# Four graph layers on one core: k's fourth product by quarters, layer 1's statistics on ScalarE, sums written in place, and a new order of work

## The chip, the cores and the metric

One core of a Trainium2 chip runs the whole kernel. The metric is the device time of one launch in microseconds (us), the median of several runs; the host is not in it. The engines are called by short names: PE is TensorE's matmul, PEld its weight load, DVE is VectorE, ACT is ScalarE, POOL is GpSimd, SP is SyncE, which issues the DMAs. All data are float32.

## The reference, cut to what matters

`x` is 128 graphs of 128 nodes with 512 features, `adj` one 128x128 matrix that all graphs share. Each of the four layers ends in a residual sum and a layer norm over the 512 features:

```python
x = layernorm(x + L0(x, adj, w0, bias))   # norm_adj @ (x @ w0) + bias
x = layernorm(x + L1(x, adj, adj, b))     # see below
x = layernorm(x + L2(x, adj, wq, wk, wv)) # rel = adj.T * (q k^T), rows scaled to norm 1, then rel @ v
x = layernorm(x + L3(x, w3, a, beta, adj))# h = x @ w3; softmax attention over leaky_relu sums; elu
```

With both weights equal to `adj`, L1 adds one value to all 512 features of a row, and the norm behind it takes that away again. So the kernel has no step for L1: its first norm stands for the norms of layers 0 and 1 (a guard with `1.0 + EPS` and `EPS * EPS` in place of `EPS`). "Layer 1's statistics" in this text are the mean and variance of that norm, the kernel's kind `w`.

## The kernel before

The 128 graphs are worked in 32 groups of four (`GB = 4`). In a group, `x(b)` is a 128x512 tile of nodes by features for graph `b`. The main work is four dense products with 512x512 weights, each called by a letter:

- `w`: the aggregate `y` (nodes summed by the normalised adjacency, steps `y..`) times `w0`; added onto `x` by steps `dw..`
- `z`: the turned `x` (`xT`) times `gq`, which is Wq and Wk multiplied once in the setup; then `pr` (steps `r0` to `r3`) and `rel` (`rm`)
- `v`: `xT` times the turned Wv; then `f`/`fa`, rel times v, added onto `x`
- `k`: the turned `x` before layer 3 (`nT`) times `w3`; then `h`, attention times k, and `em`, `ee`, `ea`

Each of these products is a 2x2 block product done with seven block products in place of eight (steps `1` to `7`, in the order 1 2 5 6 7 4 3 or near it). Sums of the left blocks (`sy`, `sx`, `sn`, four each, `Left.sum`, on POOL) and of the weights (once, in the setup) are made ahead. A block product is four matmuls of 128x256 on PE (line 766). Some of the block products are themselves done the same way one level down, "by quarters": seven 128x128 matmuls in place of eight (line 730, `make_small`). That costs: four more small sums on POOL (`Left.small`, steps `l..`), a second PE step that runs after the first (`w18` follows `w1`), a copy between the two on ACT (`b..`, `before`), and three small DVE operations (`e..`, `between`). Before the change `w` and `k` do products 1, 2 and 5 by quarters, `z` and `v` also product 4. PE executes each float32 matmul as two records, so a block product is 8 records, one by quarters 8 and 6.

Then come the norms. The first norm's statistics are on DVE (`stw0` to `stw3`, lines 965 and 966: `bn_stats` and `bn_aggr`); `gw` on ACT makes the guard (lines 1021, 1025), `pow` on POOL the inverse root (line 588) and the shift (line 585), `apw0` to `apw3` on ACT apply it (line 1029). The other two norms take their sums from `fa` and `ea` (an accumulated output), and the squares on ACT (`qv..`, `qk..`, line 1003, which write unneeded values into a dead tile). The turned `x` comes from 32x32 transposes on DVE (`xt`, `nt`, line 674) and an exchange of 16 DMAs (`xd`, `nd`, line 680). The attention tile goes through DRAM (`at`, `aw`, `cat`), as does `rel` (`rt`, `wr`, `cr`).

The order of all steps is written out in the source: a list `HEAD`, then the list `TURN` fourteen times, each time for groups one further on (a turn is one group's worth of every step, taken from six different groups), then `TAIL`. Every engine runs its share of the list in that order and waits at each instruction for its inputs. In `TURN` the number ahead of the dot is the group, relative: `4.w1` starts product `w` of a group, the `z` and `v` steps are those of the group before it (3), `2.` and `1.` are still older. The string tables `SLOTS` say which buffer each new tile takes. The left sums have seven buffers, the small attention tiles (tag `m`) four.

Of the kernel before, what the change touches and what calls it, by code (L numbers as in the profile page):

```python
# [66 lines left out]
    "l1": (
        "010111010101010010101011001101001011010010110100101101001011010010110100101101001011010010"
        "110100110010110011010110100100110"
    ),  # L70
    "l2": (
        "010101010101010010110110110110110110110110110110110110110110110110110110110110110101110101"
        "01"
    ),
    "C": (
        "010101010101011010101011011011011011011011011011011011011011011011011011011011011011011010"
# [3 lines left out]
        "012100212102102012012102012102012102012102012102012102012102012102012102012102102012012010"  # L80
        "2110210"
    ),
    "m": (
        "012301202302301210320100130133212013131201310310213231201012103232120131323021213103232120"
        "131323021213103232120131323021213103232120131323021213103232120131323021213103232120131323"
        "02121310233221302022132020213201210312121203210030"
    ),
    "x": (
        "0123457869789012345768901234576890123457689012345768901234576981032"
    ),  # L90
    "q": (
        "010101010101010001001010101010101010101010101011010101010101010100101010101001010101010101"
        "010101010101010001010101010101010101010101010101010101010101010101010101010101010101010101"
        "010101010101010101010101010101010101010101010101010101010101010101010101010101010101010101"
        "010101010101010101010101010101010101010101010101010101010100010101010101010101010101010101"
        "01010101010101010101010101010101010101010101010101010101010101010101010"
# [3 lines left out]
MIDS = 4  # L100
SUMS = 7
ROOMS = {1: 2, 2: 2}
# [8 lines left out]
0.ld1 2.ld0 0.ld0 2.ld1 1.ld1 1.ld0 s.warm s.deg s.root s.nadj s.adjt s.nadjT 0.y10 0.y01 0.cy10  # L111
1.y10 0.cy01 1.y11 1.cy10 1.y01 1.cy11 0.y11 s.m012_0 1.cy01 3.ld1 s.s00 0.w2 s.m012_1 0.cy11
s.s02 0.bi10 s.m012_3 0.y00 0.bi01 2.y10 s.s01 0.cy00 2.y11 0.bi00 0.w1 s.m05_0 0.sy0 s.s03 2.y00
1.y00 0.bi11 s.m05_1 1.cy00 0.sy2 s.m012_2 0.w5 1.bi10 s.m05_3 0.sy3 0.dw1 s.m05_2 0.w6 0.sy1
0.dw2 s.sk0 1.ly12 s.sk2 s.g1 0.dw6 s.s30 0.w7 s.cg1 1.sy0 s.m312_0 1.bi11 0.dw7 s.m312_1 0.w4
1.bi00 0.dw5 s.bi 0.w3 s.sa1 2.cy10 0.dw4 2.cy00 s.sk1 2.cy11 s.g2 s.sa0 0.dw3 0.stw3 3.y11 1.bi01
0.stw0 s.g5 0.stw1 s.sa2 s.dg2 2.y01 s.s31 1.sy2 0.stw2 1.w2 2.cy01 s.s33 s.g6 0.gw s.sa3 1.bw2
s.m35_0 1.w1 s.cg6 0.pow 1.ew2 s.g7 1.bw1 s.m35_1 2.bi11 1.ew1 0.apw0 0.apw1 1.w28 0.xt0 1.ly5
1.w18 s.cg7 s.sk3 s.la 0.apw2 0.apw3 1.sy1 1.w5 1.dw1 3.ld0 0.xt2 s.g4 1.bw5 0.xt1 2.bi01 0.xt3
s.q11 1.w6 2.bi00 s.cg4 0.xd 1.ew5 s.mg12_0 3.bi11 1.w58 s.dg5 s.q02 s.g3 2.bi10 1.dw6 1.dw2 1.w7  # L120
s.dg3 2.ly12 s.mg12_1 1.dw7 s.mg12_3 1.w4 s.sg0 1.dw5 s.sg2 2.w2 s.sg1 4.ld0 2.w1 s.m312_3 2.bw2
s.sg3 2.ew2 2.bw1 0.z1 0.sx0 s.vt3 s.vt0 0.sx2 s.vt1 2.w28 0.cz1 1.dw4 1.sy3 s.vt2 0.z6 1.stw3
s.vd 0.sx1 1.stw2 1.w3 0.cz6 0.sx3 s.mg4_0 2.sy0 0.z5 2.ew1 1.dw3 2.sy1 0.z7 s.mg4_1 2.ly5 1.stw1
2.w18 s.mg4_3 0.cz7 0.z2 2.sy2 0.dz5 1.stw0 0.z4 0.dz2 1.gw s.mg5_0 s.mg12_2 1.pow s.mg5_2 0.z3
0.cz4 s.mg5_1 s.m35_3 1.apw3 s.mg5_3 3.y10 2.dw1 1.apw2 s.sv0 0.v1 1.apw0 3.bi10 2.dw2 1.apw1
1.xt2 s.sv1 0.v2 0.cv1 1.xt3 0.dz3 0.v6 1.xt0 0.dv2 1.xt1 0.r0 s.sv3 0.cv6 1.xd s.mv5_0 2.w5
s.mv4_0 s.mv5_1 s.mv4_1 s.sv2 0.r1 2.bw5 s.mv4_3 s.mv12_0 0.r2 2.ew5 0.r3 s.mv12_2 s.mv12_1 2.w58
s.mv5_3 s.mv12_3 0.rm 0.v7 s.q10 0.sq0 0.rt 0.sq1 2.w6 0.sq2 s.q12 0.cv7 s.q03 0.sq3 s.q00 0.rp
0.v4 s.q13 0.v5 3.cy11 s.q01 3.cy10 0.wr 2.dw6 0.cv4 4.ld1 3.sy0 s.wt0 s.s32 2.w7 2.sy3 0.cr 0.dv5
s.wt1 s.mv5_2 3.y00 1.sx0 2.dw7 0.v3 s.mg4_2 3.cy00 1.lx12 2.dw5 2.w4 s.mv4_2 0.dv3 0.f3 2.dw4  # L130
3.sy1 0.f1 2.stw2 0.f2 3.bi00 2.stw3 1.v1 0.fa3 1.lx4 0.fa2 1.z1 1.bv1 0.fa1 2.w3 1.bz1 1.ev1
1.lx5 1.ez1 0.f0 1.sx2 1.v5 2.dw3 0.fa0 1.z18 1.sx3 1.bv5 2.stw0 1.v18 0.mnv 1.cz1 1.ev5 1.z5
1.sx1 0.qv2 1.z6 2.stw1 0.qv1 1.cv1 0.qv0 1.z2 1.cz6 1.v6 1.bz2 0.qv3 1.ez2 1.bz5 1.z7 0.gv 2.gw
1.ez5 0.pov 1.cv6 2.pow 1.z28 0.apv3 1.z4 1.cz7 1.dz2 0.apv0 1.z58 0.nt3 2.apw0 1.v2 0.sc00 2.apw2
0.nt0 3.y01 1.bz4 0.sc01 0.apv2 1.v58 3.bi01 1.ez4 3.cy01 1.v7 0.apv1 0.nt2 3.ly5 2.apw1 0.sc10
1.bv2 1.z48 2.apw3 0.nt1 1.v4 1.cv7 3.ly12 1.dz4 0.nd 1.ev2 3.w5 1.bv4 1.dz5 1.v28 3.bw5 0.sc11
1.z3 3.ew5 1.dv2 3.w1 0.sc20 3.w2 1.dz3 3.bw1 0.sc21 3.w58 3.ew1 1.r0 1.r1 0.sc30 3.bw2 1.ev4 1.r2
1.r3 3.ew2 1.v48 0.sc31 3.w18 1.dv4 3.w28 0.pw 3.dw1 1.rm 0.k2 0.sn0 3.dw2 1.sq0 2.xt1 1.sq1 0.sn2
0.pe 2.xt0 0.k1 1.sq2 2.xt2 1.sq3 0.sn3 2.xt3 0.k5 1.rt 0.ck1 2.xd 1.rp 1.dv5 s.m312_2 0.sn1 0.pl3
0.dk2 1.v3 0.pl0 s.m35_2 0.pl1 0.pl2 3.sy2 0.k6 1.dv3 0.ej 3.w6 0.ck6 3.sy3 0.ei 0.ex0 0.k7 3.dw6  # L140
0.ex3 0.ex2 0.ex1 3.w7 0.rd 0.ck7 0.so0 0.dk5 0.so1 4.y11 3.dw7 1.wr 0.k4 3.dw5 4.bi11 0.at 0.aw
2.lx12 3.w4 4.cy11 1.cr 0.ck4 3.w3 3.dw4 2.sx0 3.stw2 0.cat 2.z1 3.stw3 2.sx2 2.z2 3.dw3 2.bz1
3.stw0 1.f2 2.sx1 2.bz2 3.stw1 2.v1 2.lx5 2.ez2 1.f0 3.gw 0.k3 1.fa2 2.bv1 3.pow 1.fa0 2.ez1 1.f1
2.lx4 3.apw0 0.dk3 1.f3 3.apw3 3.xt0 3.apw1 2.z18 1.fa1 3.apw2 0.h0 1.fa3 2.cz1 2.v5 3.xt2 1.mnv
3.xt1 0.h3 1.qv0 2.ev1 2.z28 1.qv1 2.z6 3.xt3 1.qv2 2.dz2 3.xd 1.qv3 0.em3 2.v18 0.em0 2.bv5 1.gv
0.h1 2.cz6 2.ev5 1.pov 0.ee0 2.z7 0.ee3 0.em1 1.apv3 0.ea0 1.apv0 0.ea3 2.v58 2.cz7 2.z5 1.sc00
0.ee1 1.apv1 4.y00 1.sc01 2.bz5 0.ea1 4.y10 1.apv2 4.bi00 2.ez5 4.cy00 4.y01 4.cy10 4.bi10 1.sc10
0.h2 4.cy01 1.sc11 2.z4 4.bi01 2.cv1 0.em2 2.v2 1.sc20 2.bz4 4.sy0 0.ee2 2.z58 2.ez4 2.bv2 2.v6
4.ly12 2.ev2 1.nt1 2.z48 2.cv6 1.sc21 2.v28 2.dz4 2.sx3 2.v7 1.sc30 3.sx0 2.dz5 4.w1 1.sc31 2.cv7
3.lx12 2.dv2 2.z3 1.pw 4.bw1 1.nt2 4.ew1 2.v4 2.dz3 1.pe 4.w18 3.sx2 1.nt0 2.bv4 2.r0 1.nt3 3.lx5  # L150
4.dw1 2.r1 2.ev4 3.z2 4.sy2 0.ea2 2.r2 1.pl3 1.pl0 2.r3 4.sy1 0.mnk 1.pl2 4.w6 1.pl1 3.sx1 2.rm
0.qk3 2.rt 2.sq0 1.ej 2.v48 0.qk2 2.wr 4.dw6 3.z1 2.dv4 1.nd 2.sq1 3.lx4 0.qk1 4.w7 1.ei 2.dv5
3.bz1 1.ex0 3.ez1 1.ex1 2.v3 1.ex3 4.sy3 1.ex2 4.dw7 2.sq2 3.bz2 1.rd 2.sq3 1.so0 3.z18 3.ez2
# [254 lines left out]
def kernel(  # L408
# [43 lines left out]
    def wide(t):  # L452
        return t.rearrange("p a b -> p (a b)")
# [954 lines left out]
```

## Time and profile before

| | us |
|---|---|
| median of 4 runs (1981.95 to 1984.89) | 1982.78 |
| the profiled execution, own time | 1984.29 |
| its span, first to last instruction | 1982.5 |
| PE busy in the span | 1956.0 (99%) |
| PE busy of a 200 us window from 800 on | 200.00 |

The profile lists busy time by engine, groups of instructions by line and shape with the mean of one in ns and the idle time ahead of them, waits with what ended them, and the chain of work that ended last. PE's ends are modelled: a matmul's listed duration (379 ns for 128x256) overlaps the next one's, and what counts is how far the starts lie apart, which the chain shows. Line 579 is `copy` on ACT, 582 `tt` on DVE, 585 `pool_tt` on POOL, which record many different steps; their tile names tell them apart (`p_k`, `q_k`, `l_y`, `S_y`).

### The profile page before, as it was taken

What the parts mean: (1) busy time and instruction counts of PE and PEld (TensorE: products, weight loads), DVE (VectorE), ACT (ScalarE), POOL (GpSimd) and SP (SyncE); (2) the same over time, 40 slices, a digit from 0 to 9 for tenths busy, and PEclk for the clock granted to TensorE, in tenths of its full rate; (3) what the DMA queues carried; (4) which work ended last, traced back from release to release, by engine and by line L of the source; (5) the groups of instructions that cost most, each with busy time, mean ns of one, the idle gap of its engine ahead of it and who ended that gap; (6) DMA issues with size and microseconds to landing.
All of it is one profiled execution on the core that took longest, in us unless ns stands there. A gap on an engine that the chain in (4) does not pass through costs nothing.

```text
span 1982.5 us, 37439 instructions
## 1 busy us (share of the span) xinstructions
PE 1956.0 (99%) x12405; PEld 1724.7 (87%) x12405; DVE 1644.4 (83%) x3801; ACT 1123.9 (57%) x2800; POOL 1369.8 (69%) x1702
## 2 busy tenths in 40 slices
PE   8999999999999999999999999999999999999997
PEld 8888988888888988888988888988889888898885
DVE  7888787888788888888888888888888888787887
ACT  2245556565655656565556556556655556566467
POOL 7557678676686776786766776766877767777652
PEclk9999999999999999999999999999999999999999
DMA  5523455334444445444345453445443454434434
GB/s 203 90 47 63 97 79 135 60 85 102 107 99 85 75 90 107 104 100 74 82 91 113 98 106 57 91 99 112 92 102 59 92 106 102 96 60 108 76 73 107
DMA packets 737312, 184.55 MB, mean 93 GB/s; under 512 B 689376, under 2 KB 689760, under 8 KB 737120
## 3 DMA queue, kind: packets, MB, share of 16 engines
q1 hardware_dynamic: 736976, 182.03, 43.9%
q8 instruction: 100, 1.64, 0.4%
q14 instruction: 92, 0.75, 0.2%
q10 hardware_dynamic: 144, 0.13, 0.0%
HBM read 64.03 MB, written 49.87 MB: 57 GB/s over the span
## 4 chain that ended last, share of the span: by engine, by line
PE 89%; SPq 3%; DVE 2%; DMA 2%; POOL 2%; ACT 1%; issue 1%; POOLq 0%; DVEq 0%; ACTq 0%
PE p_k L766 10%; PE p_w L766 10%; PE p_v L730 9%; PE p_z L730 9%; PE p_v L766 8%; PE p_z L766 7%; PE p_k L730 7%; PE p_w L730 7%; PE pr L1142 5%; PE pl_k L1190 5%; PE pl_v L1190 5%; PE py L935 5%; SPq L680 3%; PE pk L1059 1%; POOL l_x L585 0%
## 5 line engine op out<-in xcount | busy, mean ns | idle before, releaser
L1029 ACT ACTIVATE x<-x,nb,r 128x512 f32<-128x512 f32 x383 | 289.6, 808 | 30.0 <-POOL nb L585 29.4
L585 POOL TENSOR_TENSOR x<-x,bias_bc 128x512 f32<-128x512 f32 x128 | 165.1, 1294 | 121.8 <-PE py L935 92.3
L588 POOL TENSOR_TENSOR r<-v,minus_half 128x4 f32<-128x4 f32 (+1 forms) x99 | 98.8, 999 | 199.7 <-ACT v L1025 188.3
L582 DVE TENSOR_TENSOR x<-p_w,x 128x512 f32<-128x512 f32 x224 | 153.5, 686 | 47.9 <-PE p_w L766 21.8
L1214 DVE SCALAR_TENSOR_TENSOR e<-x,wa_bc 128x512 f32<-128x512 f32 x256 | 172.4, 673 | 1.4 <-ACT x L1029 0.7
L579 ACT COPY C_k<-p_k 128x512 f32<-128x512 f32 x124 | 71.6, 578 | 147.3 <-PE p_k L766 134.9
L935 PE MATMUL py<-nadjT,x 128*128 128x128 f32 x1024 | 135.9, 279 | 1.5 <-DVE x L1310 0.6
L935 PEld LDWEIGHTS py<-nadjT,x 128*128 128x128 f32 x1024 | 127.9, 195 | 5.8 <-DVE x L1310 1.2
L1190 PE MATMUL pl_k<-C_k,attT 128*128 128x512 f32 x248 | 123.0, 594 | 2.0 <-DMA attT<-d_a 1.9
L1190 PE MATMUL pl_v<-C_v,relT 128*128 128x512 f32 x248 | 121.0, 593 | 0.9 <-DMA relT<-d_r 0.9
L766 PE MATMUL p_z<-S_x,gq 128*128 128x256 f32 x512 | 121.4, 380 | 0.3 <-DVE C_z L582 0.3
L766 PE MATMUL p_w<-w,S_y 128*128 128x256 f32 x512 | 121.2, 380 | 0.4 <-DVE x L582 0.4
L766 PE MATMUL p_v<-wvT,S_x 128*128 128x256 f32 x512 | 121.1, 379 | 0.0
L1305 ACT ACTIVATE pl_k<-pl_k 128x512 f32<-128x512 f32 x127 | 73.4, 581 | 82.9 <-DVE x L1302 82.1
L766 PE MATMUL p_k<-w,S_n 128*128 128x256 f32 x496 | 117.3, 379 | 0.0
L582 DVE TENSOR_TENSOR p_z<-p_z,q_z 128x128 f32<-128x128 f32 x248 | 107.3, 433 | 8.5
L582 DVE TENSOR_TENSOR p_v<-p_v,q_v 128x128 f32<-128x128 f32 x248 | 107.3, 433 | 8.5
L1199 DVE SCALAR_TENSOR_TENSOR x<-pl_v,r,x 128x512 f32<-128x512 f32 x128 | 94.5, 746 | 22.3 <-PE pl_v L1190 17.8
L766 PEld LDWEIGHTS p_z<-S_x,gq 128*128 128x128 f32 x512 | 94.1, 190 | 21.4 <-issue 5.9
L582 DVE TENSOR_TENSOR C_v<-p_v,C_v 128x512 f32<-128x512 f32 x127 | 86.4, 681 | 28.2 <-ACT C_v L579 13.5
L766 PEld LDWEIGHTS p_w<-w,S_y 128*128 128x128 f32 x512 | 93.2, 190 | 12.2 <-issue 1.1
L766 PEld LDWEIGHTS p_k<-w,S_n 128*128 128x128 f32 x496 | 91.7, 190 | 14.0 <-issue 2.9
(1627 smaller groups left out, 6244.8 us busy)
## 6 DMA issues: line engine op xcount, KB each, us to landing
x<-in_x_dram SPq DMA_DIRECT2D x64, 512.0 KB, 4.5
out_dram<-x SPq DMA_DIRECT2D x127, 256.0 KB, 2.5
d_r<-ru SPq DMA_DIRECT2D x31, 256.0 KB, 2.0
relT<-d_r SPq DMA_DIRECT2D x124, 64.0 KB, 2.6
s<-d_s SPq DMA_DIRECT2D x31, 256.0 KB, 4.1
d_a<-au SPq DMA_DIRECT2D x31, 256.0 KB, 2.4
attT<-d_a SPq DMA_DIRECT2D x124, 64.0 KB, 4.0
w<-in_L_gnn_weight_dram SPq DMA_DIRECT2D x1, 1024.0 KB, 8.9
```

The costliest lines, as they stand in the source:

```text
L582: nc.vector.tensor_tensor(o, a, b, f)
L585: nc.gpsimd.tensor_tensor(o, a, b, f)
L588: nc.gpsimd.tensor_tensor(o, v, minus_half[:, : v.shape[-1]], ALU.pow)
L730: nc.tensor.matmul(self.banks[i][:, r, bass.ts(c, P)], lhsT=lhsT, rhs=rhs, start=(not then and n == 0), stop=(n == len(steps) - 1), skip_g ...
L766: nc.tensor.matmul(ps[:, j, :], lhsT=lhsT, rhs=rhs, start=(i not in ONTO and j == 0 and kc == 0), stop=(j == 1 and kc == 1), skip_group_ch ...
L935: nc.tensor.matmul(o, lhsT=self.x_chunk(b, kc), rhs=nadjT, start=True, stop=True)
L1029: nc.scalar.activation(xt, xt, AF.Identity, bias=self.nb[k][:, b : b + 1], scale=self.rstd[k][:, b : b + 1],)
L1142: nc.tensor.matmul(self.pr[:, b, :], lhsT=self.whole["z"][:, fc, b // 2, bass.ts(b % 2, P)], rhs=self.xT.chunk(b, fc), start=(fc == 0), st ...
L1190: nc.tensor.matmul(ps, lhsT=left[:, b, :], rhs=self.whole[k][:, b, :], start=True, stop=True)
L1199: nc.vector.scalar_tensor_tensor(xt, self.pf[b], self.rnorm[:, b : b + 1], xt, ALU.mult, ALU.add, accum_out=self.total("v", b),)
L1214: nc.vector.scalar_tensor_tensor(wide(self.e), self.x(b), 1.0, wide(wa_bc[k]), ALU.mult, ALU.mult, accum_out=self.s[:, k, b : b + 1],)
L1305: nc.scalar.activation(self.pz[b], self.pz[b], AF.Exp)
```

## The change

- Product 4 of `k` is done by quarters for groups 1 to 30: `SMALL` gets `"34"`, the setup four more weight sums (`m34_0` to `m34_3`, DVE), each group steps `ln4` (four POOL sums), `k4` (four 128x128 matmuls), `bk4`, `ek4`, `k48` (three matmuls) and `dk4` in place of `k4` (four 128x256 matmuls) and `ck4`.
- The first norm's statistics move from DVE to ACT: `suw0` to `suw3` (an Identity over `x` in place with accumulated sum), `mnw` (two 128x4 operations), `qw0` to `qw3` (squares with accumulated sum, their unneeded values into `y`'s turned tile), and `gw` is left with one operation.
- `y`'s and `n`'s second left sum (`sy1`, `sn1`, the matrix S2) is written over the block that it comes from; so is the third of the small sums for single blocks, except for `x`'s block 4.
- Five buffers for left sums in place of seven, five `m` tiles in place of four, other buffers of the small sums.
- New `HEAD`, `TURN`, `TAIL` and `SLOTS`.

```diff
-    SMALL = tuple(w + i for w in "0gv3" for i in ("12", "5")) + ("g4", "v4")
+    SMALL = tuple(w + i for w in "0gv3" for i in ("12", "5")) + ("g4", "v4", "34")
...
-            self.s[n] = big.tile([P, 2, 2, P], F32, tag="S", name=f"S{n}_{self.name}", bufs=SUMS)
+            if i == 1 and self.name[0] != "x":
+                self.s[n] = A(1, 0)
+            else:
+                self.s[n] = big.tile([P, 2, 2, P], F32, tag="S", name=f"S{n}_{self.name}", bufs=SUMS)
...
-            room = big.tile([P, 4, len(i), P], F32, tag=f"l{len(i)}", name=f"l{i[0]}_{self.name}", bufs=ROOMS[len(i)])
-            s = [room[:, n] for n in range(4)]
+            over = len(i) == 1 and not (i == (4,) and self.name[0] == "x")
+            tag = "l3" if over else f"l{len(i)}"
+            room = big.tile([P, 3 if over else 4, len(i), P], F32, tag=tag, name=f"l{i[0]}_{self.name}", bufs=ROOMS[tag])
+            s = [room[:, n] for n in ((0, 1, 1, 2) if over else range(4))]
+            if over:
+                s[2] = a(1, 0)
...
+        def sum_of(self, k, b):
+            nc.scalar.activation(self.x(b), self.x(b), AF.Identity, accum_out=self.total(k, b))
+
+        def junk(self, k, b):
+            if k == "w":
+                return self.y.aT[:, b].rearrange("p a n -> p (a n)")
+            return wide(self.relT if k == "v" else self.attT)
...
-                wide(self.relT if k == "v" else self.attT),
+                self.junk(k, b),
                 self.x(b),
                 AF.Square,
...
-            if k == "w":
-                self.var_[k] = self.small("v")
-                self.nm[k] = self.small("nm")
-                nc.scalar.mul(self.nm[k], self.mv[k][:, :, 0], -1.0)
-                v, bias, f = self.mv[k][:, :, 1], eps_bc[:, 1:2], 1.0 + EPS
-            else:
-                v, bias, f = self.var_[k], eps_bc[:, 0:1], 1.0
+            v = self.var_[k]
+            bias, f = (eps_bc[:, 1:2], 1.0 + EPS) if k == "w" else (eps_bc[:, 0:1], 1.0)
```

The first part of the turn, before:

```
4.w1 3.xd 2.cv7 0.qk1 4.w2 4.ly5 2.dv4 4.bw1 1.k1 2.dv5 0.qk3 4.ew1 1.k2 4.bw2 0.gk 1.pl0 0.pok
...
3.z2 3.sx3 3.cz1 1.dk5 2.apv1 1.k4 3.lx5 2.apv2 2.nt1 2.apv0 2.nt2 3.z6 2.apv3 2.sc00 1.ck4 2.nt0
```

and after, with the stretch around the new steps and the turn's end:

```
4.w1 0.pok 1.bk2 1.pl3 1.k18 2.dv5 1.pl1 4.bw1 4.sy2 4.w28 1.ek2 0.apk3 2.v3 0.apk2 1.ln5 4.ew1
...
1.ln4 1.ex0 2.f1 1.ex3 1.ex1 4.w6 1.ex2 2.fa1 5.ld1 1.ck7 3.lx12 1.rd 5.ld0 2.f0 4.dw6 4.w5 2.fa0
4.w7 1.so0 4.bw5 2.mnv 4.ew5 2.qv0 3.sx1 3.z1 2.qv1 4.dw7 1.so1 4.w58 2.qv2 1.k4 3.sx0 2.qv3 4.dw5
3.z2 1.at 3.bz1 1.bk4 3.lx4 3.ez1 2.gv 1.aw 4.w4 1.ek4 3.bz2 2.pov 3.z18 4.dw4 1.k48 3.ez2 3.cz1
3.sx2 3.v2 2.apv1 1.dk4 2.apv2 4.w3 3.lx5 2.nt1 3.bv2 2.apv0 2.nt2 4.suw2 3.ev2 3.z28 3.sx3 3.z5
4.suw3 2.sc00 1.cat 3.z6 2.apv3 2.nt0 3.bz5 1.dk5 2.nt3 1.k3 3.cz6 3.dz2 2.nd 2.sc01 4.dw3 3.z4
2.sc10 4.suw0 3.v1 1.dk3 3.bz4 3.v28 3.ez5 4.suw1 3.z7 4.mnw 3.ez4 3.bv1 4.qw0 3.ev1 1.h1 4.qw3
3.z48 2.sc11 3.cz7 3.z58 4.qw2 1.em1 5.y00 3.dz4 4.qw1 2.sc20 3.v18 1.ee1 5.bi00 3.dz5 4.gw 5.y11
...
5.ly12 3.bv4 1.qk3 3.v7 3.ev4 2.pe 2.bk1 1.qk1 2.ek1 3.v48 1.qk2 2.sn2 5.w2 4.xd 3.cv7 5.sy0 1.gk
2.k2 3.dv4 5.bw2 5.ew2
```

## The prediction

> **What bounds the kernel now.** I read the page's first part, then the table of windows, the chain in order of time, the groups by shape, and PE's waits in the first 150 us. The first part says who is full:
>
> ```profile
> PE 1956.0 (99%) x12405; PEld 1724.7 (87%) x12405; DVE 1644.4 (83%) x3801; ACT 1123.9 (57%) x2800; POOL 1369.8 (69%) x1702
> ```
>
> The windows (busy time of PE, PEld, DVE, ACT, POOL, then the granted clock, DMA share and GB/s) say where PE is not:
>
> ```profile
> 0.00:50.00 50.00, 44.85 (x256) 40.05 (x257) 37.86 (x59) 14.09 (x25) 37.37 (x41) 1.00 0.58 205
> 50.00:100.00 50.00, 47.50 (x266) 42.02 (x265) 43.45 (x97) 12.09 (x28) 28.23 (x28) 1.00 0.53 92
> 100.00:150.00 50.00, 49.24 (x313) 43.86 (x313) 40.49 (x95) 22.08 (x55) 30.09 (x38) 1.00 0.29 43
> ...
> 1000.00:1200.00 200.00, 200.00 (x1282) 177.55 (x1281) 167.53 (x385) 116.15 (x288) 142.80 (x181) 1.00 0.46 97
> ...
> 1950.00:1983.00 33.00, 20.85 (x77) 13.88 (x75) 19.85 (x55) 24.40 (x61) 5.86 (x9) 0.85 0.34 112
> ```
>
> By the table's rows from 600 to 1600 us PE is idle for 0.1 us in all. The first 150 us lose 8.4 us, 150 to 600 lose 4.6, the last 33 lose about 11.7, where the last group's chain of small steps runs out. So a change pays by what it takes off PE, and costs what it makes PE wait. The chain (start, length, records) gives the true spacing of matmuls:
>
> ```profile
> 1009.48 1.56 PE p_z L730 x14
> 1011.04 1.73 PE p_k L766 x8
> ...
> 1047.19 1.79 PE p_w L730 x16
> ```
>
> The first line is exactly a product by quarters: 14 records in 1.56 us, 0.112 each. The second is a plain product: 8 records in 1.73, 0.216 each.
>
> **k's fourth product by quarters.** PE loses 1.73 and gains 1.56 in each of groups 1 to 30. By the last row, sixteen small records in 1.79, fourteen are 1.57, so 0.16 to 0.17 us a group, 4.9 us in all. All of it is on the path, since PE is full. Added up by these spacings, the turn is 59.98 us before (the trace repeats every 60.07) and 59.82 after.
>
> [...] The rows above have 0.112 against 0.216 for the same float32 records, nearly in proportion to the columns, so I go by the rows.
>
> The quarters' other work, by k's own rows: DVE 0.28 + 0.30 + 0.57 for the small steps and 0.68 for `dk4`, 1.83 us a group; POOL four sums of 0.457, also 1.83; ACT a copy of 0.36 for one of 0.58. The four weight sums are about 3.9 us of DVE once, spread over the head. Cover: PE's other products.
>
> **Statistics on ACT.** DVE loses 0.677 + 0.182 four times a group, 3.44 us:
>
> ```profile
> L965 DVE BATCH_NORM_STATS2 st_w<-x 128x6 f32<-128x512 f32 x128 | 86.6, 677 | 1.0
> ...
> L966 DVE BATCH_NORM_AGGREGATE mv_w<-st_w 128x2 f32<-128x6 f32 x128 | 23.3, 182 | 4.4
> ```
>
> ACT gains four sums and four squares. The squares are a known form, 0.72 and a read of 0.19, back to back 0.85. The sums are not in this trace; ACT passes over 128x512 run from 0.58 (copy out of PSUM) to 0.81 (`apply`), and I take the square's 0.72 with its read, being nearest in shape, source and accumulator. So 8 x 0.85 = 6.8 us; with the ends for the four sums (0.58 and 0.81, each with the 0.13 that a square's read adds back to back) between 6.2 and 7.2. Per turn, ACT goes from 35.2 to 42, DVE from 50.6 to 49.0, POOL from 43.2 to 45, all under 59.8. None becomes the bound by its sum.
>
> The latency does grow. After the last `dw3` two of the four DVE pairs and two small ACT steps stood ahead of the root: 2 x 0.86 + 0.49 = 2.2 us. Now two sums 1.8, `mnw` 0.4, four squares 3.6, guard 0.3: 6.1. Queued behind them on ACT are `y`'s copies, `ee1` and `apply`; behind `apply` come the transposes and the exchange. The order pays for it: `w3` starts 25.4 us into the turn, not 29.0. And the exchange does not hang on it: `xd` waits for the buffer of the older `xT`, whose last reader `v48` ends at 58.03 of 59.82, against 59.98 of 59.98. In the trace the exchange starts 0.1 us after the turn does, its sixteen issues take 11.1 us, the last lands at 12.7, POOL's `lx12` ends at 16.8, and `z1` runs at 17.3: a margin of half a microsecond that holds in every turn. In the new turn the exchange starts 1.8 us before the turn's start and `z1` is at 18.1. That wait is relaxed by over 2 us; I put the longer statistics at nothing. Without that cover each microsecond late is 32 us in all.
>
> **Sums in place, buffers, places.** The same POOL instructions with another target; the nearest in-place row (`x<-x,bias_bc`) is 1294 ns, the sums into buffers 1275, so 0 to 0.04 us a group, off the path. POOL had waited 38 us for `p_w` and 17 for `p_v` ahead of those sums; that goes, unpaid. `y`'s tile is held until the last square, but the next user of that buffer, `5.cy00`, stands behind the squares on ACT anyway. What the fewer buffers may cost shows in the places where the list leaves little room. The attention round trip loses slack: `cat` to `h1` had some 25 us, now about 8; `cat`'s issues and landings took 6.1 us (1003.9 to 1010.0). Nothing, but with 2 us to spare.
>
> **The new order's ends.** In the first 150 us DVE has 122 us of work, and PE's named waits there (us in total, times, longest) are mostly for it:
>
> ```profile
> PE p_w L766 <- DVE x L582: 2.7, 4, 0.8
> ...
> PE p_z L766 <- DMA x_0T<-sq_x: 1.2, 1, 1.2
> ...
> PE p_w L730 <- DVE p_w L582: 0.4, 1, 0.4
> ```
>
> Three groups' statistics, 10.3 us, leave DVE there and some 3 us of weight sums come. Bounds: all three waits vanish (-4.3), or the unknown order adds as much (+4.3). I take half of DVE's 3.1, -1.5. The last 33 us end on the same steps of group 31, which the quarters leave out: 0, within 1.5 either way.
>
> **The sum.** -4.9 - 1.5 = -6.4. On the profiled execution, 1984.29 (span 1982.5, 1.8 around it), that is 1977.9; it lay 1.5 over the median, so on the median 1982.78 - 6.4 = 1976.4. A measurement here can tell about 0.2%, 4 us, from no change; the limits are 1978.8 and 1986.7.
>
> **Rivals.**
> (a) The new turn makes PE wait, and the kernel is slower. Place: DVE ahead of `k48`. From `w58`'s end at 19.6 us of the turn DVE does `dw5` 0.69, `at` 0.71, `ez1` 1.15 and `ek4` 1.15, and is done at 23.3; PE wants `k48` at 23.8. `at` waits for POOL's `so1`, which I add up to 19.4 (`lx12` from 12.9, 2.9, then `so0` 1.04, `sx1` 1.28, `so1` 1.27), 0.9 before DVE is free. If POOL is over 1.4 us late, PE waits in every group, and 0.16 us a group eats the gain of the quarters, 0.3 makes it measurably slower. One microsecond a group beyond the margin gives 1982.8 - 4.9 + 30 = 2008; 0.4 us gives 1990. For it: margins of half a microsecond. Against: the old turn ran with such a margin at `z1` without one wait in 1000 us. 0.12.
> (b) Only the quarters pay, or little waits of the head eat part: 1982.8 - 4.9 = 1977.9 with nothing at the ends, 1979 to 1986 with 1 to 8 us of new waits like the `attT` ones (1.9 us between 150 and 700). The part over 1978.8 has 0.19.
> (c) The head gains more than half: all waits that DVE, POOL and DMA give between 10 and 600 us are some 10 us; with most gone, 1970. It lies within the faster share.
> (d) The quarters don't save on PE because weight loads bind (PEld 87%): then 0 for them, and the time is 1981 to 1983. Against it is the row "x14 1.56", which already has its 14 loads. 0.03, within "same".
>
> **How the numbers follow.** Faster takes the forecast and (c), 0.69; same is (b)'s rest and (d), 0.19; slower is (a), 0.12. The range runs from 1970.5, (c), to 1984.5, which leaves out (a) and (b)'s worst.
>
> **What would show it.** Right: 14 records of `p_k` for product 4 in 1.56 us; the turn's period at 59.8 to 59.9 with 200.00 busy in a 200 us window; PE's busy time near 1951; ACT near 1340 us, DVE near 1590, POOL near 1425; fewer PE waits for DVE in the first 150 us. Wrong: a period over 60.07, or a PE wait that returns every turn, at `k48` on DVE, at `h1` on `attT`, or at `z1` on `l_x`.

## The result, and the profile after

The changed kernel takes 1986.51 us (median; 1982.33 to 1989.78) where the kernel before takes 1983.40 on the same chips: 1.0015 times as long, 95% interval 1.0010 to 1.0019. The forecast was 1976.4, its range 1970.5 to 1984.5. The forecast said faster; it is 3.1 us slower, little, but the interval leaves out no change.

The page's first part, after:

```profile
PE 1952.9 (99%) x12585; PEld 1725.5 (87%) x12585; DVE 1595.9 (81%) x3669; ACT 1295.3 (65%) x3344; POOL 1424.7 (72%) x1822
```

PE's 1952.9 is near the 1951 that was forecast, DVE's and POOL's times are the forecast ones, ACT has 45 us less than forecast. So the work did what it should; the rest is where PE stood. The table of windows (PE, PEld, DVE, ACT, POOL busy, then the granted clock, DMA share, GB/s):

```profile
0.00:50.00 50.00, 41.87 (x222) 36.15 (x223) 36.13 (x47) 17.85 (x39) 38.38 (x39) 0.97 0.58 207
50.00:100.00 50.00, 47.06 (x267) 41.69 (x266) 39.78 (x84) 17.69 (x45) 23.63 (x27) 1.00 0.41 65
100.00:150.00 50.00, 49.97 (x322) 44.98 (x321) 40.83 (x91) 27.00 (x65) 30.58 (x36) 1.00 0.36 63
1000.00:1200.00 200.00, 200.00 (x1308) 178.04 (x1307) 161.70 (x375) 135.34 (x351) 151.66 (x199) 1.00 0.44 97
1950.00:1983.00 33.00, 22.47 (x81) 14.47 (x79) 21.09 (x58) 25.94 (x64) 5.96 (x9) 0.90 0.35 114
```

The middle is as full as before and does more: 1308 records in 200 us for 1282. The first row has lost 3 us of PE, and its granted clock is 0.97 where it was 1.00. That row is where most of the forecast broke. The chain of work shows one turn, between the same `pr` of two groups, and in it k's fourth product, now in two parts (`k4`, then `k48`):

```profile
1033.23 1.78 PE pr L1167 x16
...
1068.37 0.89 PE p_k L752 x8
...
1072.55 0.67 PE p_k L752 x6
...
1093.14 1.78 PE pr L1167 x16
```

The turn is 59.91 us, for 60.07 before: 0.16 a group, and 0.89 + 0.67 = 1.56 for fourteen records, both as forecast.

To see where the rest went, I split each span into PE's work and its loss. A record's spacing at full clock is 0.1116 us for 128 columns, 0.215 for 256 (the median of both traces is 0.216) and 0.430 for 512, read from these traces; what lies between the starts of two records beyond that is loss: waits, and the half clock too. The 1.4 us ahead of the first record are counted as work.

| us | before | changed | ninth head order (below) |
|---|---|---|---|
| PE's work | 1941.0 | 1936.2 | 1937.1, 0.9 of it added |
| loss, 0 to 100 us | 13.2 | 18.2 | 16.1 |
| loss, 100 to 600 | 10.6 | 7.3 | 6.0 |
| loss, 600 to 1700 | 2.4 | 3.2 | 3.7 |
| loss, 1700 to the last product | 3.8 | 7.8 | 5.9 |
| last product to the end | 11.6 | 9.6 | 9.5 |
| span | 1982.5 | 1982.3 | 1978.3 |

The work fell by 4.8 us. The head lost 5.0 more, the last groups 4.0 more less 2.0 behind the last product, and 100 to 600 us gave back 3.3. With 0.8 more between 600 and 1700 that cancels in this execution, to within 0.3 us. Between kernels that share this tail's order, the loss from 1700 us on lies anywhere from 5.9 to 9.0 in their profiles, so about a microsecond of such a row is scatter. The median of the changed kernel lies 2.2 us above its profiled execution (1984.26) and that of the kernel before 0.9 below its own (1984.29). That difference is the measured 3.1 us: the profiled execution is the fourth fastest of 42, and no trace shows what the slower ones do.

What happened in the head shows in the lists by time (start, length, engine, what). First VectorE, then PE:

```profile
24.28 1.75 DVE L530 TENSOR_TENSOR wk_t<-wk_sb 128x512 f32<-128x512 f32 x1
25.95 0.68 DVE L597 TENSOR_TENSOR x<-p_w,x 128x512 f32<-128x512 f32 x1
```

```profile
26.68 3.30 PE L788 MATMUL p_w<-w_t,S_y 128*128 128x256 f32 x8 [2.23 <-DVE x L597]
```

`w6` of group 0 waits 2.23 us for the addition `dw1`, which the new order put behind `sk0`, a sum of Wk (the first VectorE line). Then `w6`'s eight records take 3.30 us, not 1.89. The window says why, the number behind POOL's count being the clock:

```profile
27.00:30.00 3.00, 2.98 (x8) 1.85 (x6) 1.78 (x3) 0.00 (x0) 2.92 (x4) 0.53 0.64 243
```

The clock was at one half for 3.41 us from 27.20 on. PE's waits in the first 150 us (total, times, longest) have doubled in the line that was forecast to halve:

```profile
PE p_w L788 <- DVE x L597: 5.7, 5, 2.2
```

### The profile page after: what moved, and what is told of

Same layout as the page of the kernel before. It is cut to its first block, busy times and chain, and to the rows that moved or that the text cites. A ratio compares the mean times of both kernels' runs of the same rounds, so it can differ in the third digit from the quotient of the medians.

```text
span 1982.3 us, 38370 instructions
## 1 busy us (share of the span) xinstructions
PE 1952.9 (99%) x12585; PEld 1725.5 (87%) x12585; DVE 1595.9 (81%) x3669; ACT 1295.3 (65%) x3344; POOL 1424.7 (72%) x1822
## 4 chain that ended last, share of the span: by engine, by line
PE 87%; POOL 3%; SPq 2%; DVE 2%; DMA 2%; ACT 2%; issue 1%; ACTq 0%; DVEq 0%; POOLq 0%
PE p_w L788 10%; PE p_z L752 9%; PE p_v L752 9%; PE p_z L788 8%; PE p_k L752 8%; PE p_v L788 8%; PE p_k L788 7%; PE p_w L752 7%; PE py L957 5%; PE pl_v L1215 5%; PE pr L1167 5%; PE pl_k L1215 5%; SPq L702 2%; POOL x L600 1%; DMA s<-d_s 1%
## 5 line engine op out<-in xcount | busy, mean ns | idle before, releaser
L1023 ACT ACTIVATE x<-x 128x512 f32<-128x512 f32 x128 | 79.8, 625 | 57.8 <-DVE x L597 56.9
L597 DVE TENSOR_TENSOR C_v<-p_v,C_v 128x512 f32<-128x512 f32 x127 | 86.9, 685 | 36.4 <-ACT C_v L594 16.7
L597 DVE TENSOR_TENSOR p_k<-p_k,q_k 128x128 f32<-128x128 f32 x240 | 103.8, 433 | 8.3
L788 PEld LDWEIGHTS p_v<-wvT,S_x 128*128 128x128 f32 x512 | 93.0, 190 | 12.7 <-ACT C_v L594 1.5
L594 ACT COPY C_z<-p_z 128x512 f32<-128x512 f32 x97 | 56.6, 583 | 67.2 <-PE p_z L788 36.0
L597 DVE TENSOR_TENSOR C_z<-p_z,C_z 128x512 f32<-128x512 f32 x127 | 86.6, 682 | 14.7 <-PE p_z L788 9.8
L1284 ACT ACTIVATE e<-e,nmax 128x128 f32<-128x128 f32 x128 | 49.8, 391 | 73.5 <-DVE nmax L1278 73.5
```

The costliest lines, as they stand in the source:

```text
L597: nc.vector.tensor_tensor(o, a, b, f)
L788: nc.tensor.matmul(ps[:, j, :], lhsT=lhsT, rhs=rhs, start=(i not in ONTO and j == 0 and kc == 0), stop=(j == 1 and kc == 1), skip_group_ch ...
L1023: nc.scalar.activation(self.x(b), self.x(b), AF.Identity, accum_out=self.total(k, b))
```

## The experiments

The theory after this reading: quarters and statistics are worth what was forecast, and the head's order takes it back, by waits and by the half clock after them. The rivals: the quarters save less, the statistics cost something, the tail is the place, or the head moves nothing. Ratios are to the kernel before on the same chip; each is uncertain by about 0.0009, 1.8 us. Medians of different runs mix in the chips, on which the kernel before takes from 1982.1 to 1983.5. In the orders, `s.` marks a step of the setup, the number ahead of a dot the group; `dw` are the additions that empty a product's bank, `sk`, `sa`, `sg` and `s3` sums of weights.

**Quarters undone (e1).** k's fourth product in one piece again, in the same places; its weight sums, quarter sums and correction go. 

```
-4.bk4  ek4  k48 (quarters)
+4: 8 matmuls n_4 x W3_4, 128x256, in k4's place
```

> The changed kernel with the quarters alone undone: k's fourth product is four 128x256 matmuls again in every group, at the same place of the order, without its small sums, its copy, its three DVE steps and the four weight sums. Theory 'ends' (the quarters save 0.16 us a group on PE as forecast, and the loss sits in the head and the tail of the new order): a turn of 60.05 to 60.1 us in place of 59.91, 4.9 us more on PE, less 1 to 2 us of DVE in the tail and up to 2 in the head, so 1988 to 1990. Rival 'quarters' (their extra steps on DVE, ACT and POOL cost more than PE gains): faster than the changed kernel, 1981 to 1984.

Measured: 1993.69 us, ratio 1.0057 (1.0044 to 1.0069). PE's work is 1940.9, so the quarters take 4.7 off it, against 4.9 in the forecast. The time is above the 1988 to 1990 expected: the turn is 60.45 for 59.91, and on top of 0.17 of work 0.38 us are lost once a turn before a product of v, which waits for an addition, in an order that was made for the quarters. The rival that they cost more than they save falls.

**Statistics back on VectorE (e2).** 

```
-suw: sum on ScalarE; mnw, qw: mean, squares
+suw: bn_stats, bn_aggr on VectorE; mnw, qw: nothing
```

> The changed kernel with the first norm's statistics alone put back on DVE (bn_stats and bn_aggr at the places of the sums; no squares, no mean step). Theory 'ends': the move was free in the turn, so the period stays 59.91 unless DVE now is late (it gains 3.4 us a turn and is at 52.4 of 59.9): 1985 to 1990, with group 0's statistics 4 us shorter but on the busy DVE of the head. Rival 'statistics' (the longer chain on ACT makes waits at the ends): 1981 to 1984.

Measured: 2046.77 us, ratio 1.0326 (1.0311 to 1.0340), far outside both expectations. The turn is 62.20; PE waits for VectorE in each, in this order:

```profile
PE p_k L788 <- DVE C_k L597: 2.9, 3, 1.0
PE p_z L752 <- DVE p_z L597: 1.5, 3, 0.5
```

(window 1000 to 1200 us, where the changed kernel's list of waits is empty). In this order VectorE has no room for its 3.4 us a group, while ScalarE's longer chain makes no wait in the turn. The loss before 100 us is no lower either, 20.6 for 18.2. So the move to ScalarE is not what costs the time; that it costs nothing at the ends isn't shown, since VectorE's load moved with it.

**First head order (e3).** 

```
- ... s.sk0 1.ly12 0.dw1 s.sk2 0.w6 s.s30 ... 0.dw6 0.dw2 0.w7 s.sk1 ... 0.dw7 s.s33 0.w4 1.sy0 0.dw5
+ 0.dw1 (behind 2.y00) ... 0.w6 1.bi01 0.dw6 0.dw2 s.sk0 0.w7 ... 0.dw7 s.sk2 s.s30 s.m05_3 0.w4 s.sk1 1.bi00 0.dw5
```

> The changed kernel with one stretch of the head reordered: on DVE group 0's additions dw1, dw6, dw2, dw7 and dw5 go ahead of the weight sums (sk0, sk2, s30, m05_3, sk1, s31, s33) that stood in front of them. Theory 'ends': PE's waits of 2.2, 0.8 and 1.4 us between 24 and 35 us shrink to under 1.5 in all, and the 3.4 us at half clock that followed them go; 4 to 5 us less, 1981 to 1983, and with less scatter from run to run if the half clock is what differs between runs. Rival 'head moves nothing' (what PE starts earlier it waits for later, at the x exchange or the weight sums that are now later): within 1 us of the changed kernel, 1985.5 to 1987.5.

Measured: 1987.24 us, ratio 1.0022 (1.0013 to 1.0032): no gain. The wait before `w6` is gone and one of 4.62 us stands before `w3`, which waits for `dw5`, now behind slow sums; the half clock lasts 10.24 us. The rival, that the head moves nothing, held here. Whether it moves nothing in any order was open.

**The tail's order (e4).** `dk4` and `dk5` of groups 29 and 30 ahead of group 31's `rb` and score sums.

```
- 29.dk4 30.k48 30.ck7 31.rb 29.dk5 30.ei 29.k3 31.sc11 ... 31.sc20 30.ex2 30.dk5 31.sc21 30.k3
+ 29.dk4 30.k48 30.ck7 29.dk5 30.ei 29.k3 30.dk4 ... 30.dk5 30.ex1 31.rb 30.ex2 31.sc11 30.k3 31.sc20 31.sc21
```

> The changed kernel with one stretch of the tail reordered: on DVE the block sums of groups 29 and 30's k (dk4, dk5) go ahead of the restoring of w3 (rb) and of three attention sums of group 31 (sc11, sc20, sc21). Theory 'ends': PE's waits of 1.4 and 1.2 us ahead of the two k3 products shrink to under 0.5, and 1 to 2 us of it reach the end: 1984.5 to 1985.5. Rival 'DVE's sum bounds the tail' (it is busy without a gap from 1933 to 1950 whatever the order): the same time within 0.5 us, 1986 to 1987.

Measured: 1985.21 us, ratio 1.0010 (1.0001 to 1.0019), which can't be told from the changed kernel. PE's waits from 1930 us on, in this kernel:

```profile
PE pk L1084 <- DVE x L1327: 1.2, 1, 1.2
PE ps L1158 <- DVE e L1239: 1.0, 1, 1.0
PE p_k L752 <- DVE p_k L597: 0.8, 2, 0.6
PE p_k L788 <- DVE C_k L597: 0.3, 1, 0.3
```

The changed kernel has 2.2 us in the last of these lines and 0.3 in the third. There VectorE is busy for 16.50 of the 17 us from 1933 to 1950, so its order there says little more than who waits.

**The same fault put into the kernel before (e8).**

```
- 0.sy3 0.dw1 s.m05_2 0.w6 0.sy1 0.dw2 s.sk0 1.ly12 s.sk2 s.g1 0.dw6
+ 0.sy3 s.m05_2 s.g1 s.sk0 0.dw1 0.w6 0.sy1 0.dw2 1.ly12 s.sk2 0.dw6
```

> The kernel before, with one piece of the changed kernel's head order put into it: dw1 of group 0 stands behind g's sum sk0, which waits for Wk to land at about 21.8 us, and g1 goes ahead of w6. Nothing else is changed. Theory 'head': TensorE gets a wait of 2 to 4 us for VectorE ahead of w6, the granted clock falls to half for at least 3.4 us after it, the loss before 100 us rises from 13.2 to 16 us or more, and the time rises by 2 to 5 us, to 1985 to 1988. Rival 'the head is forgiving': the later start is made up by later waits getting shorter, and the time stays within 1 us of the kernel before.

Measured: 1986.32 us, ratio 1.0015 (1.0005 to 1.0024): the changed kernel's ratio, with its placing of `dw1`, `sk0` and `g1` alone. The wait is longer than the changed kernel's, 4.73 us for 2.23, and stands one product earlier, ahead of `g1`, whose eight records take 3.78 us at the half clock, not 1.97:

```profile
28.64 3.78 PE L766 MATMUL p_g<-wk_sb,wq_sb 128*128 128x256 f32 x8 [4.73 <-DVE x L582]
```

The loss before 100 us rises by 7.2 us and the time by 2.8: over 4 us are made up later. The rival, a forgiving head, falls.

**The waits filled (e7).** Transposes of the identity on PE, results unread, ahead of `w6`, `w7` and `w4`.

```
+ s.fill4 0.w6 ... s.fill2 0.w7 ... s.fill3 0.w4     (fillN: 4N transposes, 128x128)
```

> The changed kernel with 36 extra transposes of the identity on TensorE (results never read) in the places where its head waits: 16 ahead of w6, 8 ahead of w7, 12 ahead of w4 (about 0.11 us each: 1.8, 0.9 and 1.3 us, where the waits were 2.39, 1.20 and 1.51). Group 0's products come no earlier. Theory 'clock': the half granted clock (3.41 us from 27.2 in the changed kernel, 6.8 and 10.2 us in two of its variants) follows from TensorE having stood idle; with the gaps filled the granted clock stays full after the first 15 us, the stretch costs nothing, and the time falls by 1.5 to 4 us to 1982.5 to 1985, with less scatter. Rival 'clock is not tied to the gaps': the half-clock stretch is still there, the time stays at 1986 to 1988 or rises, since the extra transposes delay the products by up to 1 us.

Measured: 1983.13 us, ratio 1.0005 (0.9996 to 1.0014). No half clock before the last product, and a median 3.4 us under the changed kernel's (2.0 by the ratios), though products come no earlier. The two ratios' intervals overlap, so the gain isn't certain.

**Second to fifth head orders (e5, e9 and e10, e11, e12).** Each takes away the longest waits of the one before. e5: the sums of layer 3's weight go to 110 to 135 us, `dw1`, `dw5`, `dw2` behind the first products.

```
+ 2.y00 0.dw1 0.dw5 0.dw2 ... 0.w6 0.w3 0.dw6 0.w7 1.bi01 s.sk0 0.dw3 2.y11 ... 0.dw7 0.w4 s.sk2 s.sa0 ... 0.dw4 s.sk1
+ (at 0.r0 to 0.v5) s.s30 s.s31 s.s33 s.m35_0 s.m312_0 ...
```

> The changed kernel with its head reordered twice over: all the sums of layer 3's weight (s30, s31, s33 and the smaller ones made from them, twelve steps that nothing needs before about 190 us) go from 28 to 60 us to about 110 to 135 us; group 0's additions dw1, dw5 and dw2 stand right behind its first products, w3 goes ahead of w7, and g's sums sk0, sk2, sk1 stand behind dw6, dw7 and dw4. Nothing is added or left out. Theory 'head': the changed kernel's loss before 100 us (18.2 us of TensorE not issuing, against 13.2 in the kernel before) comes from group 0's additions standing behind slow sums, one of which waits for layer 3's weight to land at about 28 us; with these out of the way the waits of TensorE for VectorE before w6, w7, w4 and w3 (2.39, 1.20, 1.51 us) shrink to below 1.5 us in all, no stretch of half granted clock follows, the loss before 100 us is at most 14 us, and the time is 1979 to 1983 us, at or below the kernel before. Rival 'moved again', as in the first reordering: another wait takes the place, the loss stays at 18 us or more, the time at 1985 to 1988. Rival 'displaced': the twelve sums now delay the first groups' attention between 110 and 200 us, the loss of the second 100 us grows by 3 us or more and the time is above 1986.

Measured: 1986.09 us, ratio 1.0011 (1.0002 to 1.0020). VectorE's waits for `x` are down to 1.2 us; GpSimd's took their place, the loss before 100 us is 19.8, and the rival 'moved again' held:

```profile
PE p_g L788 <- POOL S_wq L600: 6.2, 2, 5.0
```

e9: Wq's sums first on GpSimd; e10: the same with e4's tail.

```
+ 0.w6 0.w3 s.g1 0.bi00 0.dw6 ... s.sa0 s.sa1 s.sa2 0.w7 1.ly12
```

> The changed kernel with the second reordering of the head and two more moves, after that one's trace: there the waits before w6, w7, w4 and w3 were gone, but TensorE came to the weight products g5 and g6 before GpSimd had summed Wq for them (waits of 1.35 and 5.20 us), and the clock was halved again. Now GpSimd sums Wq (sa0, sa1, sa2) ahead of group 1's quarter sums, w6 and w3 go ahead of g1 (which waits for Wk to land), and dw6 and w7 follow g1; two of the five sum buffers swap places for it. Nothing is added or left out. Theory 'head': no wait over 1.5 us before 40 us, no stretch of half clock, loss before 100 us at most 13 us, time 1980 to 1983 us, 3 to 5 under the changed kernel. Rival 'displaced': group 1's sums, now 4 us later on GpSimd, make TensorE wait between 45 and 100 us instead; the loss stays above 17 us and the time at 1985 or above.

> The same head, and the tail's order with the additions dk4 and dk5 of groups 29 and 30 ahead of group 31's adjacency and score sums. Theory: the two places add up: the tail alone gave 1.3 us off the changed kernel's median, so this is 0 to 1.5 us below the kernel with the head alone, 1979 to 1982.5 us. Rival: VectorE has no free time between 1933 and 1950 us, so its order there only moves the wait, and the two kernels agree within 0.7 us.

Measured: 1986.09 and 1986.48 us, ratios 1.0010 (1.0001 to 1.0018) and 1.0016 (1.0007 to 1.0025). The tail adds nothing. In e9 the loss before 100 us is 16.7; idle stretches of 2.10 us (at 38 us) and 1.98 (at 212) have 3.41 us of half clock after each.

e11: those two stretches shortened, by order and by eight transposes ahead of `w2`, which all later heads keep.

```
+ s.dg2 s.bi ...   s.fill2 1.w2 ...   3.z18 2.f3
```

> The kernel with the third head order and three more edits aimed at TensorE's longest idle stretches. In the profiles so far the granted clock went to half for 3.41 us or a multiple after every idle stretch of TensorE of 2.06 us or more (9 of 9), after one of two at about 2.0 us, and after none of those of 1.97 us or less; the third head order still had two, 2.10 us at 38.4 (w2 of group 1 waiting for the addition dg2) and 1.98 us at 212.2 (a product waiting for a transposed tile). Now dg2 goes ahead of two slow VectorE steps, 8 extra transposes of the identity (results unread, 0.9 us) stand ahead of that w2, and z's eighth part of group 3 goes ahead of the waiting product f3 of group 2. Theory 'clock': no stretch of half clock before the last product, and the time is 1980 to 1983 us, 3 to 5 us under the changed kernel and at or under the kernel before. Rival 'waits, not clock': the idle time moved once more, another place crosses 2 us, and the time stays at 1985 to 1987.

Measured: 1982.83 us, ratio 1.0003 (0.9994 to 1.0012), 3.7 under the changed kernel (2.4 by the ratios), though one new stretch of 5.72 us, with 6.83 us of half clock, stands before `g4`. e12 takes that away:

```
+ ... s.fill2 1.w2 2.cy00 0.pow 1.sy2 2.bi00 s.sa3 ... s.g7 s.cg7 0.apw3
```

> The kernel with the fourth head order, with its one long idle stretch taken away: there TensorE stood idle for 5.72 us from 43.62, because g4 waited for a bank that ScalarE empties (cg7), ScalarE stood in cg7's way with group 0's normalization (apw), and that waited for GpSimd's 1/sigma (pow) behind group 1's sums, a bias and a sum of Wq. Now cg7 goes ahead of the normalization, and pow goes ahead of sy2, the bias of group 2 and sa3 on GpSimd. Theory 'head': no idle stretch of 2 us before the last product, no half clock, loss before 50 us at most 8 us instead of 12.1, time 1978 to 1981 us, under the kernel before by 2 to 5 us. Rival 'latency is fixed': group 0's chain to its next product has a length of its own, the idle time reappears later in the first 100 us, and the time stays at 1982 to 1984.

Measured: 1985.51 us, ratio 1.0013 (1.0004 to 1.0022). That is above what the theory and the rival gave: stretches of 3.68 and 3.15 us came up behind it, 10.2 us of half clock with them.

**Sixth and seventh (e13, e14).**

```
e13 + 1.sy2 1.ly5 s.sa3 2.bi00 ...   1.dw7 1.w58 1.dw5 s.sg3
e14 + 2.cy01 2.ly12 ... 2.bi00 2.bi10 2.bi11 2.bi01 ...   1.w4 1.sy3 2.dw1 1.dw4 0.sx2 1.w3 s.sg2 0.sx1 1.dw3 s.vt3
```

> The kernel with the fifth head order, with its two long idle stretches taken away by order alone: 3.68 us at 46.67 (w5 of group 1 waiting for a quarter sum on GpSimd that stood behind biases of group 2) and 3.15 us at 66.53 (w4 of group 1 waiting for the addition dw7 behind three sums of g's weight on VectorE). Now ly5 of group 1 and sa3 go ahead of group 2's biases on GpSimd, and dw7 and dw5 of group 1 ahead of those sums on VectorE. Theory 'head': each idle stretch was a placement; without them no half clock before the last product, loss before 100 us at most 15 us instead of 21.1, time 1979 to 1982.5 us. Rival 'latency is fixed': the head has only so much independent work, the idle time and with it a stretch of half clock come back elsewhere before 100 us, and the time stays at 1984 or above.

> The kernel with the sixth head order, whose waits before 50 us were gone (loss 7.5 us there, less than the 9.4 of the kernel before) and which still had two idle stretches, each followed by 3.41 us of half clock: 2.13 us at 52.27 (w2 of group 2 waiting for its quarter sums, behind four biases on GpSimd) and 4.51 us at 66.81 (z1 waiting for the bank that group 1's additions dw4 and dw3 empty, behind sums of g's weight and transposes of Wv on VectorE). Now those biases stand behind ly12 of group 2, and dw4 and dw3 ahead of the sums and transposes. Theory 'head': no idle stretch of 2 us is left and no half clock, loss before 100 us at most 14 us instead of 19.3, time 1977.5 to 1981 us, below the kernel before, so that the head alone explains why the change did not gain what was forecast. Rival 'the head has no more to give': another wait of the same size appears before 120 us and the time stays at 1982 to 1984.

Measured: 1982.93 us, 1.0009 (1.0000 to 1.0018), and 1983.82, 1.0005 (0.9996 to 1.0013). The first 50 us lose 7.5 and 7.8 us, less than the 9.4 before, but 50 to 100 lose 11.8 and 10.4 for 3.8: waits had moved there, and neither kernel is under the one before.

**Filled stretches (e15, e16, e17).** The sixth, fourth and seventh order with transposes in the stretches that were left.

```
e15 + s.fill3 2.w2 ... s.fill7 0.z1        e16 + s.fill9 s.g4        e17 + s.fill6 2.w28 ... s.fill3 0.z5
```

> The sixth head order with extra transposes of the identity on TensorE (results unread) in its two idle stretches: 12 ahead of w2 of group 2 (1.3 of the 2.13 us) and 28 ahead of z1 of group 0 (3.1 of the 4.51 us). The products come no earlier; only the clock can gain. Theory 'clock': no half clock before the last product, and the time falls by 2 to 3.4 us against the sixth order (two stretches of 3.41 us at half), to 1979.5 to 1981.5 us, below the kernel before. Rival 'the half clock costs little, since the products wait anyway': the time stays within 1 us of the sixth order, at 1982 to 1984.

> The fourth head order with 36 extra transposes (4.0 us) in its one idle stretch, 5.72 us ahead of g4, after which its profile showed 6.83 us of half clock. Theory 'clock': no half clock, the time falls by 2 to 3.4 us, from 1982.8 to 1979.5 to 1981 us. Rival: within 1 us of the fourth order.

> The seventh head order with extra transposes in its two idle stretches: 24 ahead of w2's eighth part of group 2 (2.7 of 3.72 us) and 12 ahead of z5 of group 0 (1.3 of 2.59 us). Its profile had one stretch of half clock, 3.41 us, and its unprofiled runs were a microsecond slower than that of the sixth. Theory 'clock': 1.7 to 3 us below the seventh order's 1983.8, at 1980.8 to 1982.1. Rival: within 1 us of the seventh order.

Measured: 1983.01, 1982.50 and 1984.09 us; ratios 1.0002, 1.0001 and 1.0008, each within 0.0009. Against their twins that is +0.1, -0.3 and +0.3 by the medians, -1.4, -0.4 and +0.6 by the ratios, each uncertain by some 2.5 us. None of the three profiles has a half clock before the last product, and no gain shows: taken together, the three rule out the 2 us or more of the theory, but not one of 1 us. In e7 the half clock may have cost up to 3 us, an estimate from its 3.4 by the medians and 2.0 by the ratios.

**Eighth and ninth (e18, e19).** e18 moves `ew2` of group 2, `dw2` and `dw3`; e19 then moves group 1's `dw2` and `dw6`, Wv's transposes and, to make room, some sums of g's weight.

```
e18 + 2.w2 2.bw2 2.ew2 s.sg0 ...   2.dw1 2.dw2 1.dw4 0.sx2 1.w3 0.sx1 1.dw3 s.sg2 s.vt3 s.vt1 s.vt0 s.vt2 s.mg4_0 s.vd
e19 + 1.dw1 1.dw2 2.w2 2.bw2 2.ew2 s.sg0 1.w6 2.w28 1.dw6 2.w1 ...   2.ew1 s.vt3 s.vt1 1.dw7 1.w58 1.dw5 s.vt0 s.vt2 s.vd
```

> The seventh head order with its two idle stretches taken away by order: 3.72 us at 55.22 (w2's eighth part of group 2 waiting for the step ew2 on VectorE, behind three sums of g's weight that took 1.48 to 1.75 us each while GpSimd added six biases) and 2.59 us at 70.49 (z5 of group 0 waiting for the bank that group 2's addition dw2 empties, behind sg2 and four transposes of Wv). Now ew2 stands ahead of those sums, dw2 of group 2 behind dw1, and dw3 of group 1 ahead of sg2. Theory 'placement': loss before 100 us falls from 18.2 to 14 or less, no half clock, time 1979 to 1982 us. Rival 'the head has no more to give': the loss stays at 17 or more and the time at 1982.5 to 1984.5.

> The eighth head order, which had lost 23.2 us before 100 us in two long idle stretches (3.29 us at 56.49, group 2's w1 waiting for a bank that group 1's dw2 and dw6 empty behind three sums of g's weight; 3.71 us at 83.46, v1 waiting for the exchange of Wv's transposes, now started later) with 6.83 us of half clock after each. Now dw2 and dw6 of group 1 go ahead of those sums, and the transposes of Wv and their exchange go some 8 us earlier, as soon as their buffer is free. Theory 'placement': no idle stretch of 2 us, loss before 100 us at most 14 us, time 1979 to 1982 us. Rival 'no more to give': 17 us or more and 1982.5 or above.

Measured: e18 1987.91 us, ratio 1.0023 (1.0014 to 1.0032); e19 **1979.32 us, ratio 0.9980 (0.9971 to 0.9989)**, below both kernels: 3.2 us under the kernel before on its chip, 7.2 under the changed one's median, and its 11 runs lie within 3.0 us where the changed kernel's 42 lie within 7.5. PE's waits from 50 to 100 us, first e18:

```profile
PE p_v L788 <- DMA wvT<-sq_wv: 3.7, 1, 3.7
PE p_w L752 <- DVE x L597: 3.3, 1, 3.3
```

then e19:

```profile
PE p_w L788 <- DVE x L597: 2.3, 1, 2.3
PE p_v L788 <- DVE wvT_t L530: 0.9, 1, 0.9
```

The two differ by nothing but these few places in the order, and by 8.6 us. e18 is slower than either of its expectations: one of its two long waits, for the exchange of Wv's transposes, came of its own moves. e19's loss before 100 us was expected at 14 or less and is 16.1 in its profile, which is its longest run (1980.96) and has one wait of 2.3 us with 6.83 us of half clock. So the time came as the theory 'placement' had it, the loss did not: it lies between the theory and the rival, above the 13.2 of the kernel before. What is shown is that the order of the head alone moves the time by 8.6 us, and that the changed kernel's loss is not one that every order must keep. No run put the larger number of buffers back, but e19 has the changed kernel's few, so they don't force it. That the head's best order has been found isn't shown.

## Why the prediction was wrong, step by step

- **k's fourth product, -4.9: right.** Fourteen records take 1.56 us and the turn is 0.16 us shorter, 4.8 in thirty; counted by the spacings it is 4.7 against e1.
- **Weight loads bind (rival d): fell,** by the same 0.16 us.
- **Statistics on ACT, 0: right in the turn.** 200.00 us busy of 200. The load was put too high: the sum takes 0.625, not 0.72, and sums follow each other every 0.62 us and these squares every 0.71, not every 0.85, since the read lies under the next one. The squares of the other two norms, which all go into one dead tile, still follow every 0.85; why is not shown. ACT gained 171 us, not 216. Sums and squares in the head, and the long form:

```profile
40.12 0.61 ACT L1023 ACTIVATE x<-x 128x512 f32<-128x512 f32 x1
40.65 0.19 ACT L1023 ACTIVATION_READ_ACCUMULATOR x<-x 128x1 f32 x1
...
41.15 0.72 ACT L1033 ACTIVATE y_0T<-x,neg 128x512 f32<-128x512 f32 x1
41.78 0.19 ACT L1033 ACTIVATION_READ_ACCUMULATOR y_0T<-x,neg 128x1 f32 x1
41.87 0.70 ACT L1033 ACTIVATE y_0T<-x,neg 128x512 f32<-128x512 f32 x1
```

```profile
L1033 ACT ACTIVATE attT<-x,neg 128x512 f32<-128x512 f32 x124 | 89.6, 723 | 1.1
...
L1023 ACT ACTIVATE x<-x 128x512 f32<-128x512 f32 x128 | 79.8, 625 | 57.8 <-DVE x L597 56.9 <-DMA wvT<-sq_wv 0.7
```

- **A wait in every turn (rival a): did not come.** PE's list of waits from 1000 to 1200 us is empty.
- **"I take half of DVE's 3.1, -1.5": the step that failed.** It reckoned with VectorE's load and not with where each addition stands. The loss before 100 us rose by 5.0, that of the 150 us that the step spoke of by 3.9 (14.8 to 18.7): 5.4 off, and close to the upper bound given, +4.3. What the step left out could be read in the change's own list: `0.dw1` behind `s.sk0`, a sum that takes 1.75 us here, where the seven of its shape that ran in this trace while GpSimd rested took 0.68. That such a placing is enough, e8 shows: it costs the kernel before 2.8 us. Rival b had the mechanism (new waits in the head) and the size, 1 to 8 us, though its 1986 was just passed, and too little chance.
- **The tail, 0 within 1.5: wrong by 2.0.** 4.0 more loss from 1700 us on, 2.0 less behind the last product. The two waits before `k3` are new, 1.19 and 1.01 us; e4 moved the additions that they wait for ahead and gained nothing that can be told, so what would remove them is open.
- **150 to 600 us were not in the sum.** They gave 2.0 back, which nothing had foreseen; 600 to 1700 took 0.8.
- **Profile and median.** Of the 10.1 us between forecast and result these terms make 6.4, in the profiled executions (1984.26 against 1977.9). The other 3.7 is the step from profile to median: the forecast took off 1.5, and the changed kernel's median lies 2.2 above its profile. 0.6 of it is the baseline, 1982.78 from four runs and 1983.40 from sixty. What the rest is stays open.

With e19's head half of the 6.4 us comes out: 1979.32 against 1982.52 on the same chip. Of its profile's span, 4.2 us under the kernel before's, 3.9 is work; its head still loses 2.9 us more than the kernel before's and its last groups 2.1 more, and 100 to 600 us (4.6) and the end (2.1) make up for that. What also stays open is how much of the changed kernel's 2.2 us between profile and median is the half clock. In its runs the time goes with the mean granted clock, median 1985.2 at 0.999 and 1987.0 at 0.997, but e15 to e17 took the half clock away and no gain showed. A version with e19's head and a better tail was not tried.

## What to carry to other kernels

A load table says whether an engine can be the bound, and nothing of a stretch in which another engine waits for one small step of it: when an order changes, go through the queue ahead of each step that PE waits for, with that stretch's durations and not the turn's. One wait removed often brings up the next behind it, so an order is judged by the time and the whole head's loss, not by the wait that it took away: the first eight reorderings gave from 1.4 us worse to 3.7 better, the ninth 7.2 (by the ratios 1.6, 2.4 and 6.9). Split the span into work and loss by stage before asking why: here the work fell as forecast, and only the loss needed explaining.

## What the runs showed of the hardware

- **The clock falls after short stand-stills.** In the twenty traces, from 12 us to the last product, no idle stretch of PE between 0.95 and 1.97 us was by itself followed by a half clock, 7 of 10 between 1.98 and 2.6 us were (among them 2.23 us in the changed kernel, 2.13 in e13 and 2.34 in e19; 2.59 in e14 was not), and all 12 of 2.9 us and more (3.15 in e12 and 5.72 in e11 among them); it starts 2.3 to 4.8 us after the stretch begins (2.91 in the changed kernel; once 1.0, with a shorter stretch just ahead) and lasts 3.41, 6.83 or 10.24 us. Why the start varies these runs don't show.
- **VectorE's sums of two SBUF tiles mostly slow down while GpSimd works.** The same 128x512 sum (the first and the third line), VectorE first, GpSimd's list after it:

```profile
13.67 0.68 DVE L530 TENSOR_TENSOR w_t<-w,w_t 128x512 f32<-128x512 f32 x1
14.27 1.49 DVE L546 TENSOR_TENSOR m<-w,m 128x256 f32<-128x256 f32 x1
15.69 1.76 DVE L530 TENSOR_TENSOR w_t<-w,w_t 128x512 f32<-128x512 f32 x1
```

```profile
14.10 1.39 POOL L600 TENSOR_TENSOR y_0T<-y_0T 128x512 f32<-128x512 f32 x1 [2.83 <-ACT y_0T L594]
15.44 1.45 POOL L600 TENSOR_TENSOR x<-x,bias_bc 128x512 f32<-128x512 f32 x1
```

0.68 us before GpSimd starts and 1.76 once it runs, 2.6 times; the additions `x<-p_w,x`, with one input in PSUM, stay at 0.68 (0.65 to 0.69 for the 131 in this trace that lie wholly under GpSimd instructions). In the twenty traces, of the weight sums that lie wholly under GpSimd instructions 368 of 475 took over 1.2 times their time alone (23 of 29 in the changed kernel, 21 of 31 in the kernel before), and of 583 that ran while GpSimd rested none did (25 and 22 of them in these two). That is why a weight sum ahead of an addition costs so much in the head: `sk0` takes 1.75 us there.
